# Two half squares, separate logarithm and exponential steps, and another instruction order in a two-layer kernel on one core

## The chip, the cores and the metric

The kernel runs on one core of a Trainium2 chip. A core has five engines, each with its own instruction stream: TensorE (PE) for matrix products, VectorE (DVE), ScalarE (ACT) for activation functions, GpSimd (POOL), and SyncE (SP), which here only issues transfers. They meet only where an instruction waits for a semaphore that another one raises. The metric is the time of one execution on the device in microseconds (us); lower is better. The time before is a median over three runs.

## The reference, cut to what matters

The input `x` has shape (16, 32, 128, 128) in float32. Two layers follow, each of the form `x = x + layer(groupnorm(x))`.

```python
# layer 0: attention over channels; its matrices are small, the rows are long
q, k, v = proj(gn(x), Wq), proj(gn(x), Wk), proj(gn(x), Wv)      # 2 x 8 heads of 64
attn = softmax(einsum('bin,bjn->bij', q, k) * scale)
x = x + proj(einsum('bnj,bjd->bnd', attn, v), Wout, bout)

# layer 1: windows of 8 x 8 pixels, four small networks
def fastkan(x, ws, wb, bb):
    ln = (x - mean(x)) * rsqrt(var(x) + 1e-5)                    # per row of 16 or 32
    basis = exp(-((ln[..., None] - GRID) / DENOM) ** 2)          # 8 centres
    return flat(basis) @ ws.T + silu(x) @ wb.T + bb
y = layernorm(windows(gn(x)))
z = fastkan1(turned(y)) + fastkan2(y by width) + fastkan3(y)
x = x + fastkan4(z) + windows(gn(x))
```

So each of the four networks needs a mean, a variance, the power -1/2 of the variance, eight Gaussian bumps and nine small matrix products.

## The kernel before, in words

Layer 0 is folded into one matrix for each of the two batch halves. A first phase sums products of the input with itself (`gram_load`, `gram_turn`, `gram_sum`). From these sums the task `attention`, a long chain of small steps that goes back and forth between PE, DVE and ACT (L750 to L1022), works out the matrix. It runs twice, once for each half.

Then 64 units follow (32 for each half), each a tile of 128 partitions by 1024 elements. A unit passes through many small tasks that overlap with those of other units. `layer0_norm` applies the matrix (L1067), evicts the sum (`xh`, L1077), centres it (L1084), squares it (`n`, L1094) and asks `rsqrt_rows` for the power -1/2 of the variances. `centre` copies the centred rows (`xc`, L1104). `rows_norm` scales them (`yy`, L1139) and lets POOL finish them (L1143, L1147). `move`, `move_silu` and `move_back` rearrange tiles by transfers on SP's queue (L1187, L1176, L1379).

The networks are done in pairs: "a" holds the first and second, "b" the third of one unit and the fourth of an earlier unit. Each pair goes through the same tasks on tiles of 128 by 2048:

- `norm` (L1194 to L1222): 16 matrix products take off the mean (PE, L480); two evictions of 1024 columns (`yc`, L1204); a square of all 2048 columns (`u<-yc`, L1207); `rsqrt_rows`; then 16 or more matrix products spread the row factors again (`rb`, L1213).
- `rsqrt_rows` (L1028 to L1045): matrix products sum the squares (L1035); ScalarE takes Ln (L1043) and then Exp with scale -0.5 in place (L1044), both of 128 by 128.
- `scale` (L1224 to L1232): two products on DVE (L1230) with `rb`, which lies in PSUM.
- `seed` (L1234 to L1258): ScalarE computes the first bump or two by Square (L1245) and Exp (L1257), and the ratio `R` by Exp (L1248).
- `ladder` (L1260 to L1281): DVE gets each further bump from the one before with one instruction (L1276, 2048 columns; L1273, 1024 columns). For one bump of pair a, POOL does half: `assist`, with `att` at L1291 and the product at L1296.
- `products` (L1307 to L1340): PE multiplies the silus (L500) and eight bumps, the levels 0 to 7 (L480), into an accumulator X. Pair b also adds the results of pair a in two groups, `straight` (L1453) and `turned` (L1477); between them POOL writes a single column, the tick (L1465).

`evict_a` (`ad`, L1366), `evict_z` (`z`, L1389) and `result` (L1536) empty the accumulators. PSUM holds two Y tiles and two X tiles; SBUF holds six `u` tiles.

What sets the order: each task is a generator that yields a step, an engine with a planned duration and the tiles it takes. The class `Flow` replays these steps and decides which instruction each engine gets next; the program's order on each engine is the order in which it does so. In the steady part it follows the dictionary `ORDER`. An entry `norm_b.6.4` means step 6 of the task `norm_b`, for the unit that is 4 behind. Steps that aren't listed, such as those of `attention`, are put in where their planned start comes first. So a planned duration changes the order in the start phase, but it doesn't change what an instruction does.

Of the kernel before, what the change touches and what calls it, by code (L numbers as in the profile page):

```python
# [11 lines left out]
AF = mybir.ActivationFunctionType  # L12
# [35 lines left out]


LAG = 0.2  # L50
HOP = 0.2
LANDING = 2.5
PATIENCE = 3.0
# [3 lines left out]

ORDER = {
    "PE": (
        "products_b.9.5 norm_b.6.4 products_b.10.5 products_b.11.5 layer0_norm.2.2 products_a.0.4 layer0_norm.4.2 "  # L60
        "products_a.2.4 products_a.3.4 products_a.4.4 products_a.5.4 norm_a.0.3 products_a.6.4 products_a.7.4 "
        "norm_b.0.3 products_a.8.4 products_a.9.4 rows_norm.0.2 norm_a.4.3 products_b.0.4 norm_a.6.3 "
        "products_b.2.4 products_b.3.4 products_b.4.4 products_b.5.4 norm_b.4.3 products_b.6.4 layer0_norm.0.1 "
        "products_b.7.4 products_b.8.4 "
    ),
    "ACT": (
# [3 lines left out]
    ),  # L70
    "DVE": (
        "result.0.7 ladder_a.1.4 ladder_a.2.4 ladder_a.3.4 ladder_a.4.4 ladder_a.5.4 ladder_b.0.4 ladder_b.1.4 "
        "rows_norm.1.2 ladder_b.2.4 scale_a.0.3 ladder_b.3.4 scale_a.1.3 ladder_b.4.4 ladder_b.5.4 ladder_b.6.4 "
        "ladder_a.0.3 scale_b.0.3 scale_b.1.3 "
    ),
    "SP": (
        "move_silu.0.3 move.0.2 load.0.0 keep.0.1 store.0.6 move_back.0.3 again.0.5 "
    ),
    "POOL": (
        "rows_norm.3.2 assist.1.3 products_a.1.3 products_b.1.3 rows_norm.2.1 assist.0.2 "  # L80
# [8 lines left out]
def step(engine, us, *take, lag=None):  # L89


    return engine, us, take, LAG if lag is None else lag


class Flow:
# [158 lines left out]
def conv_preact_kernel(  # L254
# [20 lines left out]
    RB = 8 * W  # L275
# [3 lines left out]
    ACT = nc.scalar.activation  # L279
# [190 lines left out]
    def l0col(bp, kk, i):  # L470
        return l0c[:, bp, kk, i : i + 1]
# [31 lines left out]
    def layers():  # L503
        with ExitStack() as es:
# [29 lines left out]
            give, put, used = fl.give, fl.put, fl.used  # L534
# [185 lines left out]
            def gram_sum():  # L720
# [5 lines left out]
                for m in range(NBP * STEPS):  # L726
# [5 lines left out]
                    for b in range(4):  # L732
                        yield step("PE", 0.57, lag=0.0)
                        first, last = i == 0 and b == 0, i == STEPS - 1 and b == 3
                        for k, q, lo, hi in strips:
# [7 lines left out]
                            )  # L743
                    put(("summed", m), None, LAG)
                    if i == STEPS - 1:
                        put(("gram", bp), g, LAG)
                for kind in ("R", "R", "u", "u", "yy", "ad"):
                    give(kind)

            def attention(bp):  # L750
# [136 lines left out]
                for mm in range(KK):  # L887
# [140 lines left out]
            def rsqrt_rows(src, e, kind):  # L1028

                parts = e.shape[1]  # L1030
                lr, ve = yield step("PE", 0.24 * parts, kind, "Y")
                for j in range(parts):
                    for c in range(4):
                        u = parts * c + j
                        MM(  # L1035
                            ve[32 * c : 32 * c + 32, 0, 0:P],
                            lhsT=e[:, j, :],
                            rhs=src[:, u * P : (u + 1) * P],
                            start=j == 0,
                            stop=j == parts - 1,  # L1040
                        )
                yield step("ACT", 0.62)
                ACT(lr, ve[:, 0, 0:P], AF.Ln, bias=EPS)  # L1043
                ACT(lr, lr, AF.Exp, scale=-0.5)  # L1044
                give("Y")  # L1045
                return lr

            def load(n):
# [11 lines left out]
            def layer0_norm(n):  # L1060
                bp, kk, j = units[n]
                yield "get", ("matrix", bp)
                xr = yield "get", ("x", n // 2)
                xh, xp = yield step("PE", 3.65, "xh", "Y")
                for u in range(2):
                    for k in range(KK):
                        MM(  # L1067
                            xp[:, u, :],
                            lhsT=pts[bp][:, k, kk * P : (kk + 1) * P],
                            rhs=xr[:, k, u * 512 : (u + 1) * 512],  # L1070
                            start=k == 0,
                            stop=k == KK - 1,
                        )
                used(("x", n // 2), "x", 2)
                yield "get", ("layer0", bp)
                yield step("ACT", 1.06)
                ACT(xh, flat(xp), AF.Identity, bias=l0col(bp, kk, C_XB), scale=l0col(bp, kk, C_R2))  # L1077
# [13 lines left out]
                used(("xh", n), "xh", 2)  # L1091
                put(("yp", n), yp, LAG)
                sq, = yield step("ACT", 0.94, "n")
                ACT(windows(sq), chunks(yp), AF.Square)  # L1094
                used(("yp", n), "Y", 2, LAG)
                lr = yield from rsqrt_rows(sq, e0, "lr0")
                give("n")
                put(("lr0", n), lr)

            def centre(n):  # L1100

                yp = yield "get", ("yp", n)
                xc, = yield step("ACT", 1.01, "xc")
                nc.scalar.copy(windows(xc), chunks(yp))  # L1104
                used(("yp", n), "Y", 2)
                put(("xc", n), xc)
# [87 lines left out]
            def norm(name, n, wt, rhs, e, then):  # L1194

                if (name, n) != ("a", 0):
                    yield "get", ("centred", "b" if name == "a" else "a", n - 1 if name == "a" else min(n, N - 1))
                v, *yt = yield step("PE", 1.1, "yc", "Y", "Y")
                tiled(lambda q, g_: yt[g_ // 2][32 * q : 32 * q + 32, g_ % 2, :], wt, rhs, True, True)
                then()  # L1200
                put(("centred", name, n), None)
                for i in range(2):
                    yield step("ACT", 0.92, lag=0.0)
                    ACT(v[:, i * RB : (i + 1) * RB], flat(yt[i]), AF.Identity)  # L1204
                    give("Y", LAG)
                sq, = yield step("ACT", 1.81, "u")
                ACT(sq, v, AF.Square)  # L1207
                lr = yield from rsqrt_rows(sq, e, "lr")
                give("u")
                rb = yield step("PE", 1.0, "Y", "Y")  # L1210
                for j in range(4):
                    for q in range(4):
                        MM(  # L1213
                            rb[q // 2][:, q % 2, j * P : (j + 1) * P],
                            lhsT=back[name][32 * q : 32 * q + 32, j, :],
                            rhs=lr[32 * q : 32 * q + 32, :],
                            start=True,
                            stop=True,
                        )
# [464 lines left out]
```

## Time and profile before

| what | value |
|---|---|
| median of three runs | 2648.94 us (2644.55 to 2655.05) |
| the profiled execution's own time | 2646.42 us |
| its span, first to last instruction | 2644.5 us |
| start of the first `result` instruction on DVE (L1536) | 373.8 us |
| start of the last one | 2629.8 us |
| starts of two `result`s in the steady part | 1820.40 and 1856.36 us |

A profile line names the time or the line of the kernel, the engine, the operation, the tile written and the tiles read, the shape, and how often it occurs. In the timeline the first two numbers are the start and the duration of a merged group, and the brackets at the end hold the idle time of the engine before it and what ended it. In the list of waits the numbers are the total, how often, and the longest. PEld is the weight load of TensorE, which runs ahead of its matrix products. Consecutive instructions of ScalarE or VectorE overlap a little in the records, so the distance from start to start, called the pitch here, is what an instruction costs its engine.

### The profile page before, as it was taken

How to read it: one execution, taken by the hardware profiler on the slowest of the kernel's cores; microseconds unless marked ns; L12 is line 12 of the kernel's file. 1: busy time of each engine (PE TensorE's matmuls, PEld its weight loads, DVE VectorE, ACT ScalarE, POOL GpSimd, SP SyncE). 2: the span in 40 equal slices, each digit the busy share in tenths (PEclk: the TensorE clock that was granted, in tenths of full speed). 3: DMA queues.
4: the chain of work that ended last, by engine and by line, in shares of the span. 5: the costliest groups of instructions: out<-in, count | busy, mean ns of one | idle time of the engine just before them, and what ended most of it. 6: DMA issues, size and time to landing. Idle time of an engine off the chain costs nothing.

```text
span 2644.5 us, 126397 instructions
## 1 busy us (share of the span) xinstructions
PE 2505.3 (95%) x57375; PEld 1300.0 (49%) x57375; DVE 2460.2 (93%) x1697; ACT 2306.0 (87%) x1969; POOL 704.8 (27%) x559
## 2 busy tenths in 40 slices
PE   6998999999999999999999999999999999999875
PEld 6884544444444444444444444444444444444431
DVE  4755899999999999999999999999999999999977
ACT  0007699999999999999999999999999999999973
POOL 4301132232222332232332222322223322323300
PEclk9998999999999999999999999999999999999998
DMA  9752345555555555555555555555555555555521
GB/s 245 193 152 65 106 118 151 147 145 152 144 147 151 155 144 149 145 148 155 145 146 156 139 147 155 153 146 146 147 146 156 142 146 149 146 149 158 140 74 45
DMA packets 306613, 379.86 MB, mean 144 GB/s; under 512 B 42912, under 2 KB 240032, under 8 KB 306080
## 3 DMA queue, kind: packets, MB, share of 16 engines
q1 hardware_dynamic: 292728, 352.22, 48.8%
q10 hardware_dynamic: 9640, 17.11, 2.5%
q8 instruction: 453, 7.42, 1.2%
q0 software_dynamic: 3712, 2.46, 0.4%
q14 instruction: 80, 0.66, 0.1%
HBM read 103.18 MB, written 67.11 MB: 64 GB/s over the span
## 4 chain that ended last, share of the span: by engine, by line
PE 51%; DVE 12%; DMA 10%; ACT 9%; issue 7%; POOL 5%; SPq 5%; DVEq 0%; ACTq 0%; POOLq 0%
PE X L480 25%; DVE u L1276 9%; POOL att L1291 5%; PE X L500 5%; PE Y L1035 4%; DMA out<-xh 4%; PE Y L480 4%; PE X L737 3%; ACT R L1248 3%; PE Y L1213 3%; ACT u L1245 2%; PE Y L1067 2%; ACT z L1389 2%; PE Y L1128 2%; PE X L1477 2%
## 5 line engine op out<-in xcount | busy, mean ns | idle before, releaser
L1276 DVE SCALAR_TENSOR_TENSOR u<-R,u 128x2048 f32<-128x2048 f32 x781 | 1818.4, 2352 | 39.1 <-ACT u L1257 9.7
L480 PE MATMUL X<-u,wt_a 32*32 32x512 f32 x16384 | 666.6, 600 | 12.0 <-ACT u L1257 8.6
L480 PE MATMUL X<-u,wt_b 32*32 32x512 f32 x16896 | 601.4, 600 | 14.3 <-DVE u L1276 12.8
L480 PEld LDWEIGHTS X<-u,wt_a 32*32 32x32 f32 x16384 | 318.1, 103 | 226.2 <-issue 126.3
L1291 POOL TENSOR_SCALAR att<-R 128x1024 f32<-128x1024 f32 x64 | 278.4, 4350 | 548.3 <-ACT R L1248 548.3
L1245 ACT ACTIVATE u<-yc,vec 128x2048 f32<-128x2048 f32 x195 | 391.1, 2006 | 31.0 <-DVE yc L1230 16.1
L1257 ACT ACTIVATE u<-u 128x2048 f32<-128x2048 f32 x195 | 371.0, 1903 | 2.1
L1230 DVE TENSOR_TENSOR yc<-yc,Y 128x1024 f32<-128x1024 f32 x260 | 310.0, 1212 | 18.1 <-PE Y L1213 17.7
L480 PEld LDWEIGHTS X<-u,wt_b 32*32 32x32 f32 x16896 | 206.5, 103 | 237.6 <-issue 104.2
L1320 POOL MEMSET vec<- 128x1 f32 x130 | 12.8, 98 | 1138.9 <-PE X L500 1136.9
L1204 ACT ACTIVATE yc<-Y 128x1024 f32<-128x1024 f32 x260 | 250.0, 1012 | 39.3 <-PE Y L480 38.7
L1248 ACT ACTIVATE R<-yc,vec 128x2048 f32<-128x2048 f32 x130 | 259.6, 1997 | 0.0
L1207 ACT ACTIVATE u<-yc 128x2048 f32<-128x2048 f32 x130 | 247.4, 1904 | 2.2
L1067 PE MATMUL Y<-x,pt 128*128 128x512 f32 x512 | 238.5, 609 | 0.0
L737 PE MATMUL X<-R 128*64 128x193 f32 (+3 forms) x2048 | 153.1, 310 | 24.8 <-DVE R L711 24.3
L1067 PEld LDWEIGHTS Y<-x,pt 128*128 128x128 f32 x512 | 92.9, 191 | 144.4 <-issue 141.0
L737 PEld LDWEIGHTS X<-R 128*64 128x64 f32 x2048 | 142.2, 141 | 39.1 <-DVE R L711 26.3
L1296 POOL TENSOR_TENSOR u<-att,u 128x1024 f32<-128x1024 f32 x64 | 151.9, 2374 | 2.6 <-DVE u L1276 1.4
L1143 POOL TENSOR_SCALAR yy<-yy,vec,col_r 128x1024 f32<-128x1024 f32 x64 | 111.8, 1747 | 147.7 <-DVE yy L1139 125.9
L1366 ACT ACTIVATE ad<-X,col 128x1024 f32<-128x1024 f32 x128 | 135.7, 1120 | 0.8 <-PE X L480 0.6
L500 PE MATMUL X<-sd,ws_a 32*32 32x512 f32 x2048 | 95.8, 598 | 33.3 <-ACT z L1389 18.4
L480 PE MATMUL Y<-yy,c 32*32 32x512 f32 x1056 | 125.2, 598 | 0.4 <-ACT yc L1204 0.4
(222 smaller groups left out, 2929.9 us busy)
## 6 DMA issues: line engine op xcount, KB each, us to landing
xh<-xh SPq DMA_DIRECT2D x512, 128.0 KB
d<-yy SPq DMA_DIRECT2D x512, 128.0 KB
sd<-S SPq DMA_DIRECT2D x512, 128.0 KB
ad_r<-ad SPq DMA_DIRECT2D x512, 128.0 KB
x<-in_x SPq DMA_DIRECT2D x256, 128.0 KB
out<-xh SPq DMA_DIRECT2D x508, 64.0 KB
u<-in_x SPq DMA_DIRECT2D x28, 256.0 KB
u<-in_x ACTq DMA_DIRECT2D x28, 256.0 KB
```

The costliest lines, as they stand in the source:

```text
L480: MM(dst(to, g_), lhsT=wt[32 * g_ : 32 * g_ + 32, :], rhs=rhs(g_, to ^ cross[g_]), start=start, stop=stop,)
L500: done.append(MM(dst(g_ ^ w, q), lhsT=wt[o, q // 2, :], rhs=rhs(o, q), start=start, stop=stop))
L737: MM(g[64 * q : 64 * q + 64, k, lo:hi], lhsT=t[:, b, at : at + 64], rhs=t[:, b, lo:hi], start=first, stop=last,)
L1067: MM(xp[:, u, :], lhsT=pts[bp][:, k, kk * P : (kk + 1) * P], rhs=xr[:, k, u * 512 : (u + 1) * 512], start=k == 0, stop=k == KK - 1,)
L1204: ACT(v[:, i * RB : (i + 1) * RB], flat(yt[i]), AF.Identity)
L1207: ACT(sq, v, AF.Square)
L1230: TT(v[:, o], v[:, o], flat(rb[i]), ALU.mult)
L1245: ACT(u, v, AF.Square, bias=bqs[k])
L1248: ACT(up, v, AF.Exp, bias=bp_, scale=2.0)
L1257: ACT(u, u, AF.Exp, scale=-1.0, bias=lift)
L1276: STT(t, by, BIG, at, ALU.min, ALU.mult)
L1291: nc.gpsimd.tensor_scalar(rc, by[:, 0:RB], BIG, None, ALU.min)
```

## The change

The square in `norm` is made by two instructions of 1024 columns, one after the other. In `rsqrt_rows` Ln and Exp become two steps, so that instructions of other tasks can stand between them, and the Y tile is given back after Ln in the plan. Planned durations are altered, and `ORDER` is replaced for all engines.

```diff
+DRAIN = 0.13
@@ ORDER, PE
-        "products_b.9.5 norm_b.6.4 products_b.10.5 products_b.11.5 layer0_norm.2.2 products_a.0.4 layer0_norm.4.2 "
-        "products_a.2.4 products_a.3.4 products_a.4.4 products_a.5.4 norm_a.0.3 products_a.6.4 products_a.7.4 "
-        "norm_b.0.3 products_a.8.4 products_a.9.4 rows_norm.0.2 norm_a.4.3 products_b.0.4 norm_a.6.3 "
-        "products_b.2.4 products_b.3.4 products_b.4.4 products_b.5.4 norm_b.4.3 products_b.6.4 layer0_norm.0.1 "
-        "products_b.7.4 products_b.8.4 "
+        "layer0_norm.0.2 products_b.7.5 products_b.8.5 norm_b.8.4 products_b.9.5 products_b.10.5 products_b.11.5 "
+        "layer0_norm.2.2 products_a.0.4 layer0_norm.4.2 products_a.2.4 products_a.3.4 products_a.4.4 "
+        "products_a.5.4 norm_a.0.3 products_a.6.4 products_a.7.4 norm_b.0.3 products_a.8.4 products_a.9.4 "
+        "rows_norm.0.2 norm_a.5.3 products_b.0.4 norm_a.8.3 products_b.2.4 products_b.3.4 products_b.4.4 "
+        "norm_b.5.3 products_b.5.4 products_b.6.4 "
@@ ORDER, ACT
-        "seed_a.0.4 norm_b.5.4 seed_a.1.4 seed_a.2.4 layer0_norm.1.2 seed_a.3.4 seed_a.4.4 evict_z.0.5 "
-        "layer0_norm.3.2 centre.0.2 seed_b.0.4 seed_b.1.4 layer0_norm.5.2 seed_b.2.4 norm_a.1.3 norm_a.2.3 "
-        "norm_a.3.3 norm_b.1.3 norm_b.2.3 evict_a.0.4 evict_a.1.4 norm_a.5.3 norm_b.3.3 silus.0.3 "
+        "silus.0.4 norm_b.6.4 seed_a.0.4 norm_b.7.4 seed_a.1.4 seed_a.2.4 layer0_norm.1.2 seed_a.3.4 seed_a.4.4 "
+        "evict_z.0.5 layer0_norm.3.2 centre.0.2 seed_b.0.4 layer0_norm.5.2 seed_b.1.4 layer0_norm.6.2 seed_b.2.4 "
+        "norm_a.1.3 norm_a.2.3 norm_a.3.3 norm_a.4.3 norm_b.1.3 norm_b.2.3 evict_a.0.4 evict_a.1.4 norm_a.6.3 "
+        "norm_b.3.3 norm_a.7.3 norm_b.4.3 "
@@ rsqrt_rows
-                yield step("ACT", 0.62)
+                yield step("ACT", 0.19, lag=DRAIN)
                 ACT(lr, ve[:, 0, 0:P], AF.Ln, bias=EPS)
+                give("Y", 0.07)
+                yield step("ACT", 0.22)
                 ACT(lr, lr, AF.Exp, scale=-0.5)
-                give("Y")
@@ layer0_norm, centre
-                sq, = yield step("ACT", 0.94, "n")
+                sq, = yield step("ACT", 0.92, "n")
-                xc, = yield step("ACT", 1.01, "xc")
+                xc, = yield step("ACT", 0.9, "xc")
@@ norm
-                sq, = yield step("ACT", 1.81, "u")
-                ACT(sq, v, AF.Square)
+                sq, = yield step("ACT", 0.92, "u", lag=0.0)
+                ACT(sq[:, 0:RB], v[:, 0:RB], AF.Square)
+                yield step("ACT", 0.92)
+                ACT(sq[:, RB:], v[:, RB:], AF.Square)
```

The lists for DVE, SP and POOL are the old ones, begun at another place of the round: on DVE the ladders, scales and results of the steady part keep their sequence, and SP's stays the same throughout. In the lists for PE, `norm_b`'s sum of squares (its step 5 now) moves from behind level 3 of `products_b` to ahead of it, and its `rb` (step 8 now) from behind level 6 to ahead of it; level k is step k + 2 up to level 5, then come `straight` (8), level 6 (9), `turned` (10) and level 7 (11).

In the start phase the planner's choice changes as a result. The second `attention` task's instructions, threaded before with eleven ladder steps (L1276), one half step (L1273) and four scales (L1230) on DVE, now stand on DVE without them from L916 to L1019; those steps follow behind. On PE the products of the same stretch stand ahead of `norm_a`'s `rb` and of the levels of `products_b` that it was mixed with. On POOL the second tick moves ahead of one L1147. The last three units have the same order on DVE and POOL, with the half squares in their places.

More of the change, by code (lines that the diff above doesn't have):

```diff
@@ L59 @@
     "PE": (
-        "products_b.9.5 norm_b.6.4 products_b.10.5 products_b.11.5 layer0_norm.2.2 products_a.0.4 layer0_norm.4.2 "
-        "products_a.2.4 products_a.3.4 products_a.4.4 products_a.5.4 norm_a.0.3 products_a.6.4 products_a.7.4 "
-        "norm_b.0.3 products_a.8.4 products_a.9.4 rows_norm.0.2 norm_a.4.3 products_b.0.4 norm_a.6.3 "
-        "products_b.2.4 products_b.3.4 products_b.4.4 products_b.5.4 norm_b.4.3 products_b.6.4 layer0_norm.0.1 "
-        "products_b.7.4 products_b.8.4 "
+        "layer0_norm.0.2 products_b.7.5 products_b.8.5 norm_b.8.4 products_b.9.5 products_b.10.5 products_b.11.5 "
[3 more added lines that the diff above has]
+        "norm_b.5.3 products_b.5.4 products_b.6.4 "
     ),
     "ACT": (
[3 rows of a table removed]
[4 rows of a table added]
     ),
     "DVE": (
-        "result.0.7 ladder_a.1.4 ladder_a.2.4 ladder_a.3.4 ladder_a.4.4 ladder_a.5.4 ladder_b.0.4 ladder_b.1.4 "
-        "rows_norm.1.2 ladder_b.2.4 scale_a.0.3 ladder_b.3.4 scale_a.1.3 ladder_b.4.4 ladder_b.5.4 ladder_b.6.4 "
-        "ladder_a.0.3 scale_b.0.3 scale_b.1.3 "
+        "ladder_b.0.4 ladder_b.1.4 rows_norm.1.2 ladder_b.2.4 scale_a.0.3 ladder_b.3.4 scale_a.1.3 ladder_b.4.4 "
+        "ladder_b.5.4 ladder_b.6.4 ladder_a.0.3 scale_b.0.3 scale_b.1.3 result.0.6 ladder_a.1.3 ladder_a.2.3 "
+        "ladder_a.3.3 ladder_a.4.3 ladder_a.5.3 "
     ),
     "SP": (
-        "move_silu.0.3 move.0.2 load.0.0 keep.0.1 store.0.6 move_back.0.3 again.0.5 "
+        "again.0.6 move_silu.0.3 move.0.2 load.0.0 keep.0.1 store.0.6 move_back.0.3 "
     ),
```

## The prediction

> **What bounds the kernel now.** I read the page first, then the windows, then one steady period engine by engine in the timeline, then the waits. The page's first line, and the window 700 to 2300 us:
>
> ```profile
> PE 2505.3 (95%) x57375; PEld 1300.0 (49%) x57375; DVE 2460.2 (93%) x1697; ACT 2306.0 (87%) x1969; POOL 704.8 (27%) x559
> ```
>
> ```profile
> 700.00:2300.00 1600.00, 1563.22 (x37534) 770.09 (x37530) 1578.68 (x886) 1566.21 (x1328) 450.69 (x310) 1.00 0.54 148
> ```
>
> In the steady stretch PE is busy 97.7%, DVE 98.7%, ACT 97.9% at full clock, so shares don't tell the bound; the waits inside one period do. The DVE timeline from one `result` (L1536) to the next, 1820.40 to 1856.36, is 35.96 us:
>
> ```profile
> 1820.40 1.39 DVE L1536 SCALAR_TENSOR_TENSOR xh<-xh,l0c,X 128x512 f32<-128x512 f32 x2
> ...
> 1837.39 2.29 DVE L1276 SCALAR_TENSOR_TENSOR u<-R,u 128x2048 f32<-128x2048 f32 x1
> 1839.59 1.22 DVE L1230 TENSOR_TENSOR yc<-yc,Y 128x1024 f32<-128x1024 f32 x1
> ...
> 1844.06 10.12 DVE L1276 SCALAR_TENSOR_TENSOR u<-R,u 128x2048 f32<-128x2048 f32 x4
> 1854.10 2.34 DVE L1230 TENSOR_TENSOR yc<-yc,Y 128x1024 f32<-128x1024 f32 x2
> 1856.36 0.74 DVE L1536 SCALAR_TENSOR_TENSOR xh<-xh,l0c,X 128x512 f32<-128x512 f32 x1
> ```
>
> No line carries a wait for another engine: VectorE is the loop that sets this period. The four ladder steps from 1844.06 take 10.12 us; four at a pitch of 2.21 would be 8.84. Two of them wait for the step just before (about 0.4 together), and 0.84 comes from GpSimd's `att`, which runs beside them: the step from 1851.05 takes 3.12, the others 2.29:
>
> ```profile
> 1849.24 4.52 POOL L1291 TENSOR_SCALAR att<-R 128x1024 f32<-128x1024 f32 x1 [8.49 <-ACT R L1248]
> 1853.82 0.10 POOL L1465 MEMSET vec<- 128x1 f32 x1
> ```
>
> ScalarE and TensorE in the same period:
>
> ```profile
> 1836.83 0.30 ACT L1043 ACTIVATE lr<-Y 128x128 f32<-128x128 f32 x1
> 1837.16 0.31 ACT L1044 ACTIVATE lr<-lr 128x128 f32<-128x128 f32 x1
> 1837.37 1.90 ACT L1207 ACTIVATE u<-yc 128x2048 f32<-128x2048 f32 x1
> ...
> 1850.86 1.18 ACT L1077 ACTIVATE xh<-Y,l0c 128x1024 f32<-128x1024 f32 x1
> ...
> 1856.29 1.11 ACT L1389 ACTIVATE z<-X,col_r 128x1024 f32<-128x1024 f32 x1 [0.40 <-PE X L480]
> ```
>
> ```profile
> 1851.43 1.14 PE L480 MATMUL X<-u,wt_b 32*32 32x512 f32 x32
> 1852.50 1.19 PE L1213 MATMUL Y<-lr,back_b 32*128 32x128 f32 x32
> 1853.97 0.66 PE L1477 MATMUL X<-ad_r,ident 64*64 64x256 f32 x8 [0.28 <-POOL vec L1465]
> ```
>
> ACT waits once a period (0.40 before `z`), PE at `turned` (L1477, 0.28, for the tick behind `att`). And from the list of waits:
>
> ```profile
> PEld Y L1213 <- ACT xh L1077: 47.5, 57, 1.1
> ```
>
> The weight load of `rb` (L1213) waits 57 times for the `xh` eviction, which frees the Y buffer. It costs nothing now, because level 6 of `products_b` (1851.43) keeps PE busy until 1852.50, while `xh` ends at 1852.04.
>
> In all, periods from the third `result` (410.7) to the sixtieth (2471.7) average 36.16, so 0.20 a period is lost to late transfers.
>
> **The change, part by part.**
>
> *Squares in halves (130 more ACT instructions).* A 2048-wide square takes 1.81 us from start to start. A 1024-wide SBUF-to-SBUF row, `sz` (L1163), is recorded at 1.04, and such instructions overlap by 0.09, so 0.95: a pair costs 1.90, +0.09, or 12 us on ACT in all. In norm_a the square started 0.14 after its place (it reads the eviction just ahead, 1.05 where 0.90 is the pitch). The first half needs only the first eviction: -0.14. Net -0.05 a period. In norm_b the halves take the places between and behind Ln and Exp.
>
> *Ln and Exp apart.* Ln to Exp is now 0.29 to 0.33, Exp to the next 0.22. With another instruction between, I price Ln at its recorded 0.28 less the same overlap, 0.19 (an estimate; the bounds are 0.31, the present pitch, and 0.13). Saved a period: 0.12 (layer 0), 0.10 (b), and 0.04 in the block Ln, half, Exp, half of norm_a. With the 0.05: **0.31 us a period on ACT**. By itself that is worth nothing, as VectorE never waits for ACT in a regular period. No DMA is moved: the queue on SP and, but for one tick at the start, POOL's order are the same.
>
> *What the interleaving delays.* Exp of norm_a now stands behind half a square. `rb_a` on PE starts 0.62 after this Exp ends (1838.09 against 1837.47). The Exp comes 0.78 later (0.19 + 0.95 + 0.31 = 1.45 from Ln's start, instead of 0.64, and Ln starts 0.03 earlier), so `rb_a` slips 0.16. `rb_a` ends 0.33 before `scale_a` (1839.59), where 0.10 is the least seen: slack 0.23. It just fits; queued behind `rb_a` are the levels of `products_b`, and behind `scale_a` the ladder.
>
> *PE's new order.* `rsq_b` moves ahead of level 3 and `rb_b` ahead of level 6. For the first nothing waits. For the second the cover named above is gone: PE reaches `rb_b` at about 1851.45 and then waits for `xh` (1852.04 less up to 0.31), some 0.3 to 0.6 us, with level 6, `turned` and level 7 queued behind it. That closes a new loop: level 7's end to `z` 0.14; `z` to the end of `xh` 31.72 now (1820.33, a period ahead of the row shown, to 1852.05), 31.41 then; 0.08 to PE; `rb_b` 1.10, level 6 1.07, `turned` 1.02, level 7 1.16. Sum **35.98**, where the same loop was 35.22 (no level 6 in it, 0.31 more ACT). That is VectorE's 35.96 with all slack spent. With Ln at 0.31 and no wait removed it is 36.4; with Ln at 0.13 and `xh` earlier it is 35.8 and hidden by VectorE. I take 35.98, because each term but Ln has its own row. Late transfers, until now partly absorbed by 0.7 us of slack, go straight into the period: between 0 and 0.2 more, I take 0.06. So 0.08 a period over 57 periods: **+4.6 us** (bounds 0 and +25).
>
> *DVE's contention.* `att` starts up to 0.31 earlier, at 1848.93 against a ladder step's 1848.84. Where it started 0.06 ahead of a step (366.19), the group of four took 10.11, as now. So 0. The Trainium skill, page "SBUF — State Buffer", section "Who interferes with whom", calls the pair of ports that VectorE and GpSimd share an exclusive lock for a whole instruction. By that rule an `att` that gets in first (2.76 us undisturbed at 2555.87) would hold the step up for all of it, about 1.9 us a period more than now, an estimated 109 us slower; the row at 366.19 shows 0.84 and decides.
>
> *The start.* The second `attention` task is now one uninterrupted chain on DVE and PE; it was threaded with 11 ladder steps, a half and four `scale`:
>
> ```profile
> 265.43 0.42 DVE L916 TENSOR_REDUCE u<-Y 128x4 f32<-128x256 f32 x1 [1.45 <-PE Y L905]
> ...
> 318.87 0.31 DVE L1019 COPY l0c<-l0c 64x1 f32<-64x1 f32 x2
> 319.21 2.29 DVE L1276 SCALAR_TENSOR_TENSOR u<-R,u 128x2048 f32<-128x2048 f32 x1
> ```
>
> Alone, its rows add up to 24.7 us: softmax 2.5, L931 1.9, evictions 1.4, L940 3.6, pt 1.7, L966 2.0, prod 0.8, the column matmuls 4.2, and 6.6 for the averages, rsqrt and coefficients. It ends at 290.1 instead of 319.2. Then the ladders it had covered run, one DVE period without `result`, 35.96 - 1.32 = 34.64: the next `scale_a` comes at 324.7, where it stood at 321.42. **+3.3 us**, nearer this than +17.8, which the first attention's 39.2 us (131.77 to 170.93, threaded with transposes) would give; below, -3 if the start fills better. I round up to +4 for hops.
>
> *The end.* The order of the last three units differs only in what is said above; three waits of 0.14 between eviction and square lie on its chain: -0.4.
>
> Sum: 4.6 + 4 - 0.4 = +8 on the profiled 2646.42 (span 2644.5 and 1.9 around it), 2654.6. The median of the runs shown is 2.5 above the profiled run, so about 2657.
>
> **The rivals.**
>
> *The new loop bites (slower).* Ln costs its present 0.31 and late transfers add 0.2: period 36.16 + 0.34, 57 times is 19, with the start 23: 2672. For it: three engines above 97.7%, slack of 0.02. Against: ACT's own rows.
>
> *Nothing happens.* VectorE hides both ends of it, the start comes out even: 2649. For it: DVE's period without a foreign wait.
>
> *The start costs more:* attention alone at up to 39.2 us, +18 with nothing else: 2667.
>
> *Faster, by one mechanism: `att` leaves the ladder's way.* A ladder step beside an `att` that began while VectorE was idle (2557.61) took 2.29, not 3.12. If ACT's 0.31 brings `att` forward far enough to lose half of the 0.84, 0.42 a period, 24 us, less 4 at the start: 2629. It must start over 0.4 us before the step, 0.5 earlier than now; ACT brings 0.31, so it falls short.
>
> **How the numbers follow.** Chances: forecast 0.42, the loop bites 0.25, nothing 0.18, the start 0.07, faster 0.08. A difference of 0.5%, 13 us, is about the least that a measurement can tell. Slower by more than that: the loop and the start, and a little of the forecast, less their low ends: 0.33. Faster: 0.09. The rest, 0.58. The forecast's own range is 2646 to 2670 (its bounds, with the runs' spread of 10 us about the median). The whole range goes from 2637, which leaves out most of the faster case, to 2682, which is the loop's case and that spread: some 0.12 is left outside it by the cases, and I keep no more than that, since Ln's price is bounded only from afar.
>
> **What would show it.** Right: PE waits at L1213's line for ACT `xh` with PE idle 0.3 to 0.6 a period; the next Ln-to-next pitch is 0.19; the pair of halves 1.90; `result` every 36.0 to 36.3; the first `result` 3 to 5 us after 373.8. Wrong: a ladder step beside `att` that is no longer 3.12, DVE waits of over 0.3 a period, or the first `result` over 8 us away.

## The result, and the profile after

The changed kernel takes 2666.65 us (median of six runs, 2664.11 to 2669.75), against 2648.47 (2644.55 to 2657.88) for the kernel before on the same chip. The ratio is **1.0065, with a 95% interval of 1.0047 to 1.0083**: slower by 0.65%, 18 us. The forecast was 2657 with a range of 2637 to 2682. So the time lies in the range, but "within 0.5%" was the likeliest case, and this is just outside it.

The profiled execution took 2666.13 us, with a span of 2664.3 (before 2646.42 and 2644.5). Its +19.8 us of span divide at three instructions of VectorE, the first, second and fifty-ninth `result` (L1541 now; the second and the fifty-ninth are the ones that the prediction counts as third and sixtieth):

| stretch | before | after | difference | forecast |
|---|---|---|---|---|
| start to the first `result` | 373.8 | 382.8 | +9.0 | +4 |
| first to second | 36.9 | 36.9 | 0 | |
| 57 periods, second to fifty-ninth | 2061.0 | 2071.0 | +10.0 | +4.6 |
| fifty-ninth to the end | 172.8 | 173.5 | +0.7 | -0.4 |

The page's first line, the shares of the chain that ended last (its section 4), and the window 700 to 2300 us:

```profile
PE 2520.6 (95%) x57375; PEld 1304.1 (49%) x57375; DVE 2465.0 (93%) x1697; ACT 2290.7 (86%) x2099; POOL 730.7 (27%) x559
...
PE 75%; ACT 6%; DVE 6%; DMA 5%; issue 3%; SPq 3%; POOL 1%; DVEq 0%; ACTq 0%; POOLq 0%
```

```profile
700.00:2300.00 1600.00, 1564.00 (x37321) 766.88 (x37316) 1572.46 (x882) 1548.08 (x1411) 470.04 (x308) 1.00 0.54 148
```

ScalarE is 18 us less busy in this window (1548.08 against 1566.21, with 83 more instructions), and VectorE 6 us less. Nothing got heavier; time was lost in waits. The regular period has hardly changed. VectorE from one `result` to the next, 2237.53 to 2273.53:

```profile
2237.53 1.41 DVE L1541 SCALAR_TENSOR_TENSOR xh<-xh,l0c,X 128x512 f32<-128x512 f32 x2
...
2256.73 1.21 DVE L1235 TENSOR_TENSOR yc<-yc,Y 128x1024 f32<-128x1024 f32 x1
...
2261.20 10.15 DVE L1281 SCALAR_TENSOR_TENSOR u<-R,u 128x2048 f32<-128x2048 f32 x4
2271.26 2.34 DVE L1235 TENSOR_TENSOR yc<-yc,Y 128x1024 f32<-128x1024 f32 x2
2273.53 1.39 DVE L1541 SCALAR_TENSOR_TENSOR xh<-xh,l0c,X 128x512 f32<-128x512 f32 x2
```

That is 36.00 by these rounded starts and 35.98 to 35.99 in regular periods, where it was 35.95 to 35.96. The group of four ladder steps takes 10.15 where it took 10.12. ScalarE, in the same period:

```profile
2253.83 0.28 ACT L1045 ACTIVATE lr<-Y 128x128 f32<-128x128 f32 x1
2254.00 1.05 ACT L1210 ACTIVATE u<-yc 128x1024 f32<-128x1024 f32 x1
2254.95 0.30 ACT L1048 ACTIVATE lr<-lr 128x128 f32<-128x128 f32 x1
2255.15 1.05 ACT L1212 ACTIVATE u<-yc 128x1024 f32<-128x1024 f32 x1
...
2267.64 1.19 ACT L1080 ACTIVATE xh<-Y,l0c 128x1024 f32<-128x1024 f32 x1
...
2273.46 1.11 ACT L1394 ACTIVATE z<-X,col_r 128x1024 f32<-128x1024 f32 x1 [0.79 <-PE X L482]
```

Logarithm to the next instruction is 0.17, half to exponential 0.95. The exponential of norm_a ends at 2255.25, behind half a square. ScalarE now waits 0.79 before `z`, where it waited 0.40: the time saved is there, and it is idle. TensorE:

```profile
2255.30 1.17 PE L1218 MATMUL Y<-lr,back_a 32*128 32x128 f32 x32 [0.17 <-ACT lr L1048]
...
2268.78 1.27 PE L1218 MATMUL Y<-lr,back_b 32*128 32x128 f32 x32
2269.97 1.14 PE L482 MATMUL X<-u,wt_b 32*32 32x512 f32 x32
...
2272.16 1.16 PE L482 MATMUL X<-u,wt_b 32*32 32x512 f32 x32
```

TensorE now stands 0.17 ahead of `rb_a` (L1218 with `back_a`), waiting for that exponential, in each of the 57 periods. `rb_b` follows `straight` at once and begins as `xh` ends (2268.83). What VectorE waited for in the 57 periods, first before and then after (line, releaser: us in total, times, longest):

```profile
DVE u L1276 <- PE X L480: 5.0, 10, 0.8
DVE yc L1230 <- PE Y L1213: 2.1, 9, 0.5
DVE yy L1139 <- PE Y L1128: 0.4, 1, 0.4
```

```profile
DVE u L1281 <- PE X L482: 5.5, 9, 2.2
DVE yc L1235 <- PE Y L1218: 5.0, 14, 0.7
DVE xh L1541 <- PE X L482: 1.8, 3, 0.7
DVE yy L1142 <- PE Y L1131: 1.6, 6, 0.5
DVE u L1281 <- DVE u L1281: 0.9, 2, 0.5
```

Three waits grew: `scale` for `rb` (the second line), `result`, and `rows_norm`. They fall in irregular periods, mostly ones in which TensorE had been held up. In the one that begins at 2055.35, TensorE stands 1.00 ahead of the products with `d` (at 2064.02), and VectorE then waits 0.54 at `rows_norm` and 0.36 at `scale`. The view names no releaser for most holds at `d`; where it does, as for one of 0.8 in e1, it is the transfer that brings `d`. All waits listed grew from 7.5 to 14.8, by 7.3 us. The 0.03 more in a regular period would be another 1.7 over 57 of them, so the two give some 9 of the 10.0.

In the start phase, VectorE, first before and then after:

```profile
207.51 2.35 DVE L1230 TENSOR_TENSOR yc<-yc,Y 128x1024 f32<-128x1024 f32 x2 [3.09 <-PE Y L1213]
```

```profile
203.19 1.22 DVE L1235 TENSOR_TENSOR yc<-yc,Y 128x1024 f32<-128x1024 f32 x1 [4.19 <-PE Y L1218]
...
225.48 1.21 DVE L1235 TENSOR_TENSOR yc<-yc,Y 128x1024 f32<-128x1024 f32 x1
233.70 2.29 DVE L1281 SCALAR_TENSOR_TENSOR u<-R,u 128x2048 f32<-128x2048 f32 x1 [7.01 <-ACT u L1262]
...
268.59 0.43 DVE L918 TENSOR_REDUCE u<-Y 128x4 f32<-128x256 f32 x1 [1.45 <-PE Y L907]
...
293.42 1.22 DVE L1235 TENSOR_TENSOR yc<-yc,Y 128x1024 f32<-128x1024 f32 x1
```

From 268.59 on, the second `attention` is one chain, 24.8 us long. But there is a second change, higher up. Before, the two halves of the `scale` at the top were one pair (L1230, at 207.51). Now the second half comes 22.3 us behind the first, behind twelve small steps of `attention` and one `rows_norm`. The seeds of the next ladder need both halves, and VectorE stands 7.01 us for them at 233.70.

### The profile page after: what moved, and what is told of

Its sections match the earlier page's. It is cut to its first block, busy times and chain, and to the rows that moved or that the text cites. A ratio compares the mean times of both kernels' runs of the same rounds, so it can differ in the third digit from the quotient of the medians.

```text
span 2664.3 us, 126585 instructions
## 1 busy us (share of the span) xinstructions
PE 2520.6 (95%) x57375; PEld 1304.1 (49%) x57375; DVE 2465.0 (93%) x1697; ACT 2290.7 (86%) x2099; POOL 730.7 (27%) x559
## 4 chain that ended last, share of the span: by engine, by line
PE 75%; ACT 6%; DVE 6%; DMA 5%; issue 3%; SPq 3%; POOL 1%; DVEq 0%; ACTq 0%; POOLq 0%
PE X L482 35%; PE Y L1070 7%; PE X L502 6%; PE Y L1037 5%; PE Y L1218 5%; PE Y L482 4%; DVE u L1281 4%; PE X L739 3%; ACT z L1394 2%; PE Y L1131 2%; PE X L1482 2%; PE X L1458 2%; DMA out<-xh 2%; DMA u<-in_x 1%; ACT u L1250 1%
## 5 line engine op out<-in xcount | busy, mean ns | idle before, releaser
L482 PE MATMUL X<-u,wt_b 32*32 32x512 f32 x16896 | 612.1, 604 | 10.2 <-DVE u L1281 8.7
L1296 POOL TENSOR_SCALAR att<-R 128x1024 f32<-128x1024 f32 x64 | 297.2, 4643 | 556.7 <-ACT R L1253 556.7
L482 PEld LDWEIGHTS X<-u,wt_b 32*32 32x32 f32 x16896 | 200.0, 103 | 233.3 <-issue 141.3
L739 PE MATMUL X<-R 128*64 128x257 f32 (+3 forms) x2048 | 150.5, 307 | 22.3 <-DVE R L713 21.9
L1210 ACT ACTIVATE u<-yc 128x1024 f32<-128x1024 f32 x130 | 137.3, 1056 | 0.1
L1212 ACT ACTIVATE u<-yc 128x1024 f32<-128x1024 f32 x130 | 136.7, 1052 | 0.0
```

What stands on the lines that cost most here:

```text
L482: MM(dst(to, g_), lhsT=wt[32 * g_ : 32 * g_ + 32, :], rhs=rhs(g_, to ^ cross[g_]), start=start, stop=stop,)
L739: MM(g[64 * q : 64 * q + 64, k, lo:hi], lhsT=t[:, b, at : at + 64], rhs=t[:, b, lo:hi], start=first, stop=last,)
L1296: nc.gpsimd.tensor_scalar(rc, by[:, 0:RB], BIG, None, ALU.min)
```

## The experiments

Each ratio is against runs of the kernel before on the same chip; there its median was 2640.23 (e1 to e4), 2644.72 (e5 to e8) and 2643.54 (e9 to e12). Edits are to the changed kernel unless said otherwise. "Chain" means a second `attention` as in the changed kernel, "threaded" one mixed with ladder steps.

| kernel | start | Exp of norm_a | PE's two steps | ratio, 95% interval | first `result` | regular period | `scale` waits for `rb`, 57 periods |
|---|---|---|---|---|---|---|---|
| before | threaded | ahead | old | 1 | 373.8 | 35.95 | 2.1 |
| changed | chain | late | new | 1.0065, 1.0047 to 1.0083 | 382.8 | 35.98 | 5.0 |
| e1 | threaded | ahead | new | 1.0030, 1.0018 to 1.0042 | 371.1 | 36.03 | none |
| e2 | threaded | late | new | 1.0022, 1.0009 to 1.0035 | 375.0 | 35.98 | 1.8 |
| e3 | chain | late | old | 1.0062, 1.0043 to 1.0082 | 383.8 | 35.95 | 4.7 |
| e4 | threaded | ahead | old | 1.0001, 0.9989 to 1.0012 | 369.7 | 35.95 | none |
| e5 | threaded | late | old | 1.0015, 1.0002 to 1.0029 | 372.5 | 35.95 | 4.1 |
| e8 | chain | ahead | old | 1.0053, 1.0034 to 1.0072 | 381.6 | 35.95 | none |

The last three columns are from one profile each. The `scale` at the top begins anywhere between 202.5 and 211.0 in these profiles, threaded or not, and the first `result` carries that with it. Counted from that `scale`, the first `result` comes after 166.2 us in the kernel before, 179.6 in the changed one, 167.1 in e4 and 178.3 in e8.

### e1: the exponential ahead of the half squares

```diff
-        "norm_b.3.3 norm_a.7.3 norm_b.4.3 "
+        "norm_a.7.3 norm_b.3.3 norm_b.4.3 "
```

> The changed kernel with the exponential of norm_a put back ahead of the two half squares of norm_b (logarithm, exponential, half, half). The planner then threads the second attention task with ladder steps again, so this run changes two things: the start and the delay of the exponential. Theory 'start': the first result comes at 373 to 376 us instead of 382.8, 7 to 9 us saved. Theory 'lost slack' (the late exponential uses up the 0.62 us that late transfers used to disappear in): TensorE's wait of 0.17 to 0.19 a period ahead of rb_a goes, VectorE's waits at scale_a fall from 0.081 a period to under 0.02, and the 57 periods from the second to the fifty-ninth result get 4 to 7 us shorter in all; total 2650 to 2655. Theory 'new loop' (the forecast's: TensorE's new places close a loop with ScalarE): the periods stay at a mean of 36.3, total 2656 to 2659.

Measured: 1.0030. The start is 11.7 us shorter in the trace, more than expected, and `scale` no longer waits. But the period got longer, 36.03 at the least, which no theory had foreseen. TensorE shows why, in one such period:

```profile
1124.23 0.63 PE L1458 MATMUL X<-ad_r,near 64*64 64x256 f32 x8
1124.78 1.65 PE L1218 MATMUL Y<-lr,back_b 32*128 32x128 f32 x32
1126.37 1.14 PE L482 MATMUL X<-u,wt_b 32*32 32x512 f32 x32
```

`rb_b` takes 1.65 where it takes 1.19 when `xh` is long done: it stands nearly half a microsecond for `xh`. That is the forecast's loop. Logarithm and exponential of norm_a follow each other directly here, which costs ScalarE 0.31 + 0.22 instead of 0.17 + 0.20, so `xh` comes later. The loop's terms add up to the period: `z` to the end of `xh` 31.50, from there to the end of level 7 4.40, to the next `z` 0.15, together 36.05. VectorE waits at `result`, the loop's end, and no longer at `scale`:

```profile
DVE xh L1541 <- PE X L482: 2.7, 8, 0.5
DVE u L1281 <- PE X L482: 0.8, 1, 0.8
```

### e2: the start alone

```diff
+EARLY = {"ACT": (
...
+    "norm_a.7.3 norm_b.3.3 norm_b.4.3 "
+)}
+ROUNDS = 5
...
-            out[engine] = [(name, m - behind, k) for m in range(units + TURNS) for name, k, behind in names]
+            first = [(name, int(k), int(behind)) for name, k, behind in (t.split(".") for t in EARLY.get(engine, text).split())]
+            out[engine] = [(name, m - behind, k) for m in range(units + TURNS) for name, k, behind in (first if m < ROUNDS else names)]
```

> The changed kernel with the exponential of norm_a ahead of the half squares in the first five rounds of ScalarE's order alone, which is enough to thread the second attention task with ladder steps; from then on the order is that of the changed kernel. Theory 'start': the first result at 373 to 376 us, the periods from the second to the fifty-ninth result unchanged (mean 36.3, waits at scale_a about 0.08 a period), total 2656 to 2660. If the start's loss is not from the threading, the first result stays near 382.8 and the total near 2666.

Measured: 1.0022, first `result` at 375.0. Against the changed kernel's 1.0065 the start alone is worth 0.43%, 11 us. The 57 periods took 2062.4 us with the same steady order that took 2071.0 in the profile above: irregular periods differ so much from one execution to the next that a single profile tells their cost only to within some 5 us.

### e3 and e4: TensorE's places

```diff
-        "layer0_norm.0.2 products_b.7.5 products_b.8.5 norm_b.8.4 products_b.9.5 products_b.10.5 products_b.11.5 "
+        "layer0_norm.0.2 products_b.7.5 products_b.8.5 products_b.9.5 norm_b.8.4 products_b.10.5 products_b.11.5 "
...
-        "norm_b.5.3 products_b.5.4 products_b.6.4 "
+        "products_b.5.4 norm_b.5.3 products_b.6.4 "
```

> The changed kernel with TensorE's two moved steps in their old places: rsq_b behind level 3, rb_b behind level 6. The start keeps its unthreaded order, first result about 383. Theory 'new loop': the periods get shorter by 0.08 to 0.17 us, 5 to 10 us in all, total 2656 to 2662, and TensorE waits for the tick ahead of turned again. Theory 'lost slack': the exponential is as late as before, TensorE still waits 0.17 a period ahead of rb_a and VectorE 0.08 at scale_a, the mean stays at 36.3, total 2664 to 2668.

Measured: 1.0062, no gain. With the exponential late, the old places don't help.

e4 has this edit and that of e1.

> Both edits: the exponential of norm_a ahead of the half squares, and TensorE's two steps in their old places. VectorE's order is then that of the kernel before from first to last, so what is left of the change is the halves and the interleaving in norm_b and layer 0. Theory 'lost slack': equal to the kernel with the exponential ahead alone within 3 us, 2648 to 2655. Theory 'new loop': 5 to 10 us faster than that one. If late transfers cost more for another reason, the mean period stays at 36.3 and the total is 2657.

Measured: 1.0001. It is 0.29% faster than e1, 8 us, as the theory of the new loop said; 5 of them are the regular period, 57 times 0.09. So TensorE's places cost nothing beside a late exponential, and 8 us beside an early one; neither theory was right alone. e4 also prices the rest of the change, the halves and the interleaving in norm_b and layer 0: nothing, though ScalarE waits 0.56 before `z` instead of 0.40. (VectorE's order is the old one there, but for one ladder step in the start.)

### e5 and e6: the exponential by doses

e5 is e3 with the early rounds of e2: against e4, only the exponential is late.

> The fourth case of the square: threaded start, TensorE's two steps in their old places, the exponential of norm_a behind the first half square of norm_b as in the changed kernel. So against the kernel with both edits only the late exponential differs. Theory 'lost slack': TensorE waits 0.17 to 0.2 a period ahead of rb_a, VectorE at scale_a 0.03 to 0.1 a period, total 4 to 7 us above the kernel with both edits, ratio to the kernel before 1.0015 to 1.003. Theory 'only TensorE's places cost' (the forecast's: the late exponential just fits): ratio 0.999 to 1.001.

Measured: 1.0015. That is 0.14% above e4, 4 us, but the two intervals overlap, so the size isn't shown. The traces show the mechanism: in the four profiles with the exponential behind one half (the changed kernel, e2, e3 and e5), `scale` waits for `rb` for 1.8 to 5.0 us in 57 periods; in the six with the changed ScalarE order and the exponential ahead (e1, e4, e7 to e10) for 0 to 0.8. The kernel before, with the whole square, has 2.1. One event can be compared directly, a hold of more than 0.4 at the products with `d`: `scale` waits 0.36 after each of the 7 in the changed kernel, 0.17 after each of the 3 in the kernel before, and not at all after the 2 in e4.

e6 puts the exponential behind the second half too:

```diff
-        "norm_b.3.3 norm_a.7.3 norm_b.4.3 "
+        "norm_b.3.3 norm_b.4.3 norm_a.7.3 "
```

> The same with the exponential of norm_a behind both half squares of norm_b, a further 0.95 us later. Theory 'lost slack': rb_a, whose end has 0.15 to 0.25 left to scale_a when the exponential is late by one half, now ends some 0.7 to 0.8 after VectorE could begin scale_a, so each regular period takes 36.6 to 36.8 and the total is 38 to 48 us above that of the kernel before. If VectorE's scale_a has more room than that, the period stays under 36.2.

Measured: 1.0186 (1.0160 to 1.0212), 49 us, median period 36.77. VectorE's waits in the 57 periods, first in e5 and then in e6:

```profile
DVE yc L1244 <- PE Y L1227: 4.1, 13, 0.6
DVE yy L1151 <- PE Y L1140: 2.6, 3, 1.6
```

```profile
DVE yc L1244 <- PE Y L1227: 50.2, 59, 1.3
DVE yy L1151 <- PE Y L1140: 1.4, 3, 0.7
```

With one half in between, `scale` waits 13 times; with two, always. Before, `rb_a` began 0.62 behind the exponential and ended 0.33 ahead of `scale`. With one half it begins 0.05 behind and ends 0.26 ahead (e5); with two, 0.05 and 0.10, the least seen. So the first half leaves 0.16, which no longer covers a hold of TensorE.

### e7: an exchange on VectorE

```diff
-        "ladder_b.0.4 ladder_b.1.4 rows_norm.1.2 ladder_b.2.4 scale_a.0.3 ladder_b.3.4 scale_a.1.3 ladder_b.4.4 "
+        "ladder_b.0.4 ladder_a.5.4 ladder_b.1.4 rows_norm.1.2 ladder_b.2.4 scale_a.0.3 ladder_b.3.4 scale_a.1.3 "
```

> The kernel with both edits, and on VectorE the last ladder step of a (ladder_a.5) behind the first of b (ladder_b.0) from the eighth round of the order on, so that the first two steps of b no longer follow each other directly. Where they do, the second waits 0.10 and the pitch is 2.39 instead of 2.21. If nothing else is late: 0.18 a period, period 35.78, 9 to 10 us less than the kernel with both edits, ratio to the kernel before 0.996 to 0.997. If TensorE's loop from z over xh to level 7 (35.9 with Exp ahead) or the later last level of a takes over: a gain of under 4 us, with VectorE's waits at result or rows_norm.

Measured: 1.0006 (0.9994 to 1.0019), and a second step of b that still waits 0.10. The planner passes over an entry that can't start yet, and it kept VectorE's order as in e4, but for two instructions near the end. So the idea wasn't tried; the run is a second measurement of e4.

### e8, e9 and e10: the start, whole and in parts

e8 is e4 with the changed kernel's ScalarE order in the first five rounds, by the same means as in e2.

> The kernel with both edits, with ScalarE's order of the changed kernel in the first five rounds alone: the second attention task is one chain again, the steady order is untouched. Theory 'start': the first result 9 to 13 us later than in the kernel with both edits, total 2648 to 2652, the 57 periods equal within 3 us. If the un-threaded start also leaves the transfers in a worse phase, the 57 periods get 5 to 10 us longer as well, total 2655 to 2660.

Measured: 1.0053, first `result` 11.9 us later than in e4; the 57 periods took 2057.5 against 2056.1. The start costs its 12 to 14 us and leaves the steady part alone.

In e9 only the fourth round has the changed kernel's order, in e10 only the fifth:

```diff
-ROUNDS = 5
+ROUNDS = (3,)
...
-            out[engine] = [(name, m - behind, k) for m in range(units + TURNS) for name, k, behind in (first if m < ROUNDS else names)]
+            out[engine] = [(name, m - behind, k) for m in range(units + TURNS) for name, k, behind in (first if m in ROUNDS else names)]
```

> The kernel with both edits, with ScalarE's order of the changed kernel in the fourth round alone. The first part of the second attention task then has the changed kernel's order (one half of a scale behind twelve of its steps), the second part is threaded as in the kernel before. If the start's loss is in both parts: the rows' maximum that opens the second part comes 3 to 6 us later, and the first result 3 to 6 us later than in the kernel with both edits. If it is all in the un-threaded second part, as the forecast had it: under 1 us.

> The complement: the changed kernel's order in the fifth round alone, so the first part is as in the kernel before and the second part is one chain. The forecast's sum for this alone is 3.3 us; with the slower ladders behind it seen in the changed kernel (36.6 us to the next scale pair instead of 34.64) it is 5 to 6. First result 3 to 7 us later than in the kernel with both edits; this run and the other together make the 12 us of the un-threaded start.

Measured: e9 1.0036 (1.0024 to 1.0048), e10 1.0019 (1.0004 to 1.0034). VectorE's opening steps, first in e9 and then in e10:

```profile
202.50 1.22 DVE L1244 TENSOR_TENSOR yc<-yc,Y 128x1024 f32<-128x1024 f32 x1 [4.19 <-PE Y L1227]
224.78 1.22 DVE L1244 TENSOR_TENSOR yc<-yc,Y 128x1024 f32<-128x1024 f32 x1
233.01 2.29 DVE L1290 SCALAR_TENSOR_TENSOR u<-R,u 128x2048 f32<-128x2048 f32 x1 [7.01 <-ACT u L1271]
...
267.76 0.42 DVE L927 TENSOR_REDUCE u<-Y 128x4 f32<-128x256 f32 x1 [1.45 <-PE Y L916]
```

```profile
202.66 2.35 DVE L1244 TENSOR_TENSOR yc<-yc,Y 128x1024 f32<-128x1024 f32 x2 [3.09 <-PE Y L1227]
...
261.92 0.42 DVE L927 TENSOR_REDUCE u<-Y 128x4 f32<-128x256 f32 x1 [1.45 <-PE Y L916]
...
286.83 1.22 DVE L1244 TENSOR_TENSOR yc<-yc,Y 128x1024 f32<-128x1024 f32 x1
```

With the split pair (e9), the rows' maximum that opens the second part comes at 267.76, with the whole pair at 261.92. The first `result` is 6.1 us later than in e4 in e9 and 5.9 in e10, 12.0 together, where e8 has 11.9 (counted from the top `scale`, 6.2 and 5.9, where e8 has 11.2). The two parts add up to within a microsecond. By the ratios, less certain, they are 9 and 5, and the whole is 14.

### e11 and e12: the loop over `rb_b` by doses

e11 is e4 with `rb_b` two places further ahead. e12 is the kernel before with `rb_b` ahead of level 6 and nothing else.

```diff
-        "layer0_norm.0.2 products_b.7.5 products_b.8.5 products_b.9.5 norm_b.8.4 products_b.10.5 products_b.11.5 "
+        "layer0_norm.0.2 products_b.7.5 norm_b.8.4 products_b.8.5 products_b.9.5 products_b.10.5 products_b.11.5 "
```

```diff
-        "products_b.9.5 norm_b.6.4 products_b.10.5 products_b.11.5 layer0_norm.2.2 products_a.0.4 layer0_norm.4.2 "
+        "products_b.9.5 products_b.10.5 products_b.11.5 layer0_norm.2.2 products_a.0.4 layer0_norm.4.2 "
...
-        "products_b.7.4 products_b.8.4 "
+        "products_b.7.4 products_b.8.4 norm_b.6.3 "
```

> The kernel with both edits, with rb_b on TensorE two places further ahead, ahead of straight and of level 6. It tests the forecast's loop (z on ScalarE, to the end of xh, rb_b, and what TensorE does behind it up to level 7) by a dose: z to the end of xh 31.50, to TensorE 0.05, rb_b 1.10, straight 1.05, level 6 1.07, turned 1.02, level 7 1.16, to z 0.14, together 37.09. Theory 'new loop': period 37.0 to 37.1, total about 64 us above the kernel before, TensorE standing some 1.5 us a period at rb_b. If the wait for xh is not what closes the loop, the period stays under 36.3.

> The kernel before with rb_b ahead of level 6 and nothing else: whole square, logarithm and exponential together. The forecast's loop with ScalarE's old 31.72 from z to the end of xh: 31.72 + 0.08 + 1.10 + 1.07 + 1.02 + 1.16 + 0.14 = 36.29. Theory 'new loop': median period 36.2 to 36.3, 14 to 19 us more over 57 periods, ratio 1.005 to 1.0075, VectorE waiting at result. If TensorE finds xh in time: ratio 0.999 to 1.001.

Measured: e11 1.0294 (1.0271 to 1.0316), median period 37.32; e12 1.0061 (1.0041 to 1.0080), median period 36.27. The longest waits of VectorE in the 57 periods, first in e11 and then in e12:

```profile
DVE xh L1541 <- PE X L482: 75.0, 57, 1.7
```

```profile
DVE xh L1536 <- PE X L480: 15.1, 57, 0.6
```

In both, VectorE waits at `result` in all 57 periods and hardly anywhere else. The loop's sum hits e12 within 0.02. It falls 0.23 short of e11, and 0.19 of that is a wait which the sum had left out: TensorE stands for the tick ahead of `turned` there in most periods. `z` to the end of `xh` took 31.49 in e11, as expected.

## Why the prediction was right or wrong

- **The halves, logarithm and exponential on ScalarE: right.** A pair of halves is 1.89 (0.947 and 0.946), forecast 1.90. The logarithm's pitch with another instruction behind it is 0.157 to 0.173, forecast 0.19. The 0.14 ahead of the square is gone. ScalarE's wait before `z` grew from 0.40 to 0.71 to 0.79, so 0.31 to 0.39 was saved, forecast 0.31. And it was worth nothing, as said.
- **"It just fits" (the late exponential): wrong.** It holds in a regular period, where `rb_a` ends 0.26 before `scale_a`, and it fails when TensorE is held up at `d`. The slack of 0.62 looked idle in a regular period; it was part of what kept such holds from VectorE. The 0.36 against 0.17 and none after a hold, and the dose in e6, show it; how many microseconds it costs, some 4, isn't clear of noise. The forecast booked late transfers against the new loop instead, at 0.06 a period.
- **TensorE's new loop: it exists, but it doesn't set this kernel's regular period.** The sum said 35.98, and 35.98 is measured, but that is chance. Where the loop closes (e1 and e12), the end of `xh` to the end of level 7 takes 4.39 to 4.40, and 0.15 more to `z`. With the 31.72 of e12 that makes 36.27, with the 31.50 of e1 36.05, both as measured, so the mechanism is right. With the 31.35 of the changed kernel it makes only 35.90. In its regular periods TensorE takes 4.49, because `turned` begins as the tick ends (0.05 behind it), and VectorE waits for nothing at `result`. Accordingly the wait of 0.3 to 0.6 at `rb_b` isn't there: TensorE reaches `rb_b` only as `xh` ends, since `straight` begins 30.20 behind `result` instead of 29.99. Part of that comes from `rb_a`, which begins 0.08 later; I didn't separate the rest.
- **The regular period's 0.03: another cause.** The third of VectorE's four ladder steps begins 2.425 behind the second, where it was 2.396. In the kernels with TensorE's new places (the changed one, e1, e2) the wait instruction ahead of it names TensorE's semaphore beside VectorE's own and is recorded at 0.050; with the old places (before, e3, e4, e5) it names one and takes 0.021. No term of the forecast had it.
- **The steady sum:** forecast +4.6. e2 minus e4, both with the threaded start, is 0.21%, some 5.5 us; the profiled execution showed 10.0. The size was about right by luck: of its two terms, the loop doesn't set the regular period, and what irregular periods cost came in part through the exponential.
- **VectorE's contention: right.** The step behind the one with which `att` starts still takes 3.12.
- **The start: wrong, and this is the step that failed.** The forecast said +4; it costs 11 to 14 (changed kernel against e2, e8 against e4). Its price for the chain was good: 24.7 us forecast, 24.8 measured. But it laid that chain onto the old beginning at 265.43 and took the ladders behind it at full pitch. The first part of the task had been re-ordered too, with one half of a `scale` pushed behind twelve small steps, and that is 6.1 us (e9), not priced at all. The second part is 5.9 (e10) instead of 3.3, since the ladders didn't run at full pitch (one step takes 3.37, and VectorE waits 0.32 and 0.31): in the changed kernel it is 36.6 us from the chain's end to the next `scale`, where the forecast took 34.64. In the profile of the changed kernel this start shows as only +9.0, because its top `scale` began 4.3 us earlier (203.19 against 207.51); the first `result` still came over 8 us late, one of the signs named for being wrong.
- **The end: wrong by 1.1 us,** +0.7 instead of -0.4. No run separates it; e4, which costs nothing in all, has 173.7 there.

The rival "the start costs more" named 2667, which is what came out, but by another mechanism: it priced one long attention, not a split `scale`. And that the time lies in the range is partly luck: the upper end, 2682, was there for the new loop, which hardly bites in this kernel, and the 8 to 10 us missing at the start fell into that room.

So of the 18 us, 11 to 14 are the start, about 5 the late exponential and TensorE's places together (not told apart beyond noise), and the halves themselves nothing. No kernel here beats the one before; e4 equals it.

## What to carry to other kernels

Slack that looks idle in a regular period may be what absorbs a hold elsewhere, such as a late transfer: before spending it, follow a late one through the chain, and don't stop at "it still fits". Where a planner fills in what isn't listed by hand, a small edit in the steady order can re-order the start-up; compare the whole start on the engine that matters, not only the stretch where the difference is obvious. And two edits that each spend slack need not add: pricing them one by one took the full square of variants.

## What the runs showed of the hardware that was not expected

- **A ladder step holds up GpSimd's `att` to its end; `att` holds up a step only for its first 0.9 us.** POOL's and VectorE's lines for the period shown above, where `att` starts just behind a ladder step:

```profile
2266.02 4.91 POOL L1296 TENSOR_SCALAR att<-R 128x1024 f32<-128x1024 f32 x1 [8.14 <-ACT R L1253]
```

```profile
2266.01 2.29 DVE L1281 SCALAR_TENSOR_TENSOR u<-R,u 128x2048 f32<-128x2048 f32 x1
```

  `att` starts 0.00 to 0.16 behind a step in most periods of the changed kernel, and 0.4 or 0.6 behind in the kernel before. Where a step that takes its 2.29 was under way, 840 times in the 14 profiles, `att` ends 4.91 to 4.94 behind the step's start, however early it began itself. So its recorded time grows with an earlier start (median 4.51, now 4.81) and its end doesn't move: it looks as if it stood until the step was over and then took the 2.77 that it takes alone. The next step takes 3.12, 0.84 more, in both kernels. In ten places of the profiles `att` starts first, by 0.01 to 0.18 (366.19 in the kernel before is one). There it takes 2.77, and the step ends 3.18 behind `att`'s start, 0.89 later than a step alone would that began with `att`; a step that begins 1.74 behind it takes 2.29 and isn't held (2557.61, before). The Trainium skill, page "SBUF — State Buffer", section "Who interferes with whom", calls the shared pair of ports an exclusive lock, has a VectorE instruction with two inputs in SBUF (a ladder step is one) contend with a GpSimd instruction that reads SBUF, and lets the order of issue decide who blocks. Where the step is first, these rows agree. Where `att` is first, it holds the step for 0.9 of its 2.77 us only, not for the whole instruction as the prediction read the page, and there the measurement decides.
- **A wait for two semaphores takes longer than one for one.** VectorE's wait instruction ahead of the ladder step named above is recorded at 0.050 with two and at 0.021 with one, and the step begins 0.03 later.
- **ScalarE's overlap depends on what follows.** A half square is recorded at 1.05 and the next instruction begins 0.947 behind its start; ahead of a table load the pitch is 1.06, so nothing overlaps. The Trainium skill, page "ScalarE: Activation LUTs", section "What ACT_TABLE_LOAD costs", gives an overlap of about 0.093 us for activations that follow each other, and the halves agree with it (0.10). The exponential that needs the logarithm just ahead of it doesn't overlap: the logarithm is recorded at 0.277 and the pitch is 0.308 in e1, where an independent instruction follows after 0.157 to 0.173.
- **`rb_b` needs `xh` only for most of itself.** In e11 and e12 its first 4 matmuls are recorded before `xh` ends and the other 28 after it; in e12 level 7 then ends 4.39 behind `xh`, where the prediction's terms, with the whole block in them, make 4.43.
